# A two-layer graph network on one core: the last edges of the first layer in batches of five and three units, the last batch's stages one step earlier, and a last node group of one block

## The chip, the cores and the metric

The kernel runs on one core of a Trainium2 chip. Its time is the device time of one execution in microseconds (us). The engines are PE (matrix multiply; its weight loads are listed apart as PEld), DVE (vector), ACT (activations), POOL (here: issuing gathers) and SP (issuing transfers). Each engine works through its own list of instructions in order, and an instruction waits until what it needs has been produced or released.

## The reference, cut to what matters

There are 6250 nodes with 128 features and 206250 edges, sorted by their target node; each node has 33 incoming edges on average, itself among them. Two layers are computed, each with a layer norm of `x + layer(x)` behind it.

The first layer is graph attention with 8 heads of 16:

```
m      = leaky_relu(xl[src] + xr[dst] + edge_attr @ W_e, 0.2)
logits = sum over o of m * att              # one number per edge and head
exl    = exp(logits - segment_max(logits, dst)[dst])
alpha  = exl / (segment_sum(exl, dst)[dst] + 1e-16)
out    = segment_sum(xl[src] * alpha, dst) + b_att
h      = layer_norm(x + out); y = layer_norm(h + gelu(h @ W1 + b1) @ W2 + b2)
```

The second layer gathers a row of features for every edge (`feat[src]`, made from the result of the first layer), multiplies it with filters that a small network makes from 8 scalars of the edge, and sums over the target node.

## The kernel before, in words

**Units.** The edge list is cut into units of 6 x 128 = 768 edges, NU = 269 of them (`TU`, `UE`). A unit spans at most 32 target nodes (`W`), so its sums go into a window of 32 columns of an accumulator `acc` that starts at the unit's first target, `r0[u]`. For this the sorted targets are checked on the chip at the start; otherwise a general version would run.

**Layer one, per unit** (`attention`): `load` issues 6 gathers of 128 rows of the table `fXL` on POOL (line 366) and five transfers on SP; `terms` adds the three terms of `m` in PSUM (lines 420, 423); `parts` and `logits` make the 48 logits of each edge row on DVE (436, 439, 445).

**Batches.** The maximum over the edges of a node needs the edges in a row. So units are taken in batches of up to 8, and four stages are done once for a batch: `rows` (SP fetches two mask tables `nb` and `hb`, PE turns the logits, line 462, ACT copies them to `lgt`), `peaks` (four scans on DVE, lines 471 to 477, and a carry `cr` from the batch before), `shifts` (`gd` and `sc` on DVE, 494 and 496) and `weights` (PE 506, 508 and 516; ACT takes the exponentials, 511 and 514). `fast_plan` makes the list of batches: 3, 4, 6 and then 32 of 8, each with its `end`, the step at which the logits of its last unit are there.

**Per unit again, behind its batch:** `one_hot` and `messages` multiply the gathered rows with the weights (DVE 372, 528), `sums` adds over edges (PE 538, ACT 542 and 543 copy to `sb`), `sum_up` (PE 551) and `collect` (DVE 557) add the unit's window to `acc`; the window's start is read by DVE's sequencer from memory (value_load, L597 in the trace).

**The order is written out by hand**: `attention` runs through steps k. Step k issues the gathers of unit k+2, the terms of unit k+1, and the logits of unit k. The dictionary `when` says at which step the messages of a unit are done (one unit in a step, two near the end, never more); its sums follow one step later, its `sum_up` two and its `collect` three. `rows` of a batch are done at step `end` + 1, `peaks` at `end` + 2, `shifts` and `weights` at `end` + 3, and the last batch's messages start at `end` + 3 (of other batches `end` + 4). With 269 units and the last batch 261 to 268 (`end` 268), rows, peaks and weights of the last batch fall in steps 269, 270 and 271, its messages in steps 271 to 274 (two units each), and there are steps 0 to 277.

**Node groups.** When a stretch of 256 nodes (two blocks of 128; the first group of all is one block) has all its sums, its remaining work on nodes is done by a generator, `nodes.group`, in 19 pieces that are separated by `yield`. Counting them: 1 the sums are taken out of `acc` (PE 675, 676), 2 division and adds (DVE 679 to 687), 3 and 4 layer norm (620 to 632), 5 scale and shift (693, 694), 6 transposition (665, 667), 7 and 8 two halves of the first product with gelu (702, 705), 9 the second product (710), 10 adds (713, 714), 11 and 12 layer norm, 13 adds (720 to 722), 14 and 15 layer norm, 16 transposition, 17 the product for layer two (733, 734), 18 the transfer to the table `fFEAT` (736, 737), 19 that to `fBASE` (741). Each piece is written for g blocks. `Queue.step` lets each group in flight do one piece. At most two groups are in flight (`lanes` = 2), each with one PSUM buffer of its own, and a third starts only when the older one has done its last piece. A group may start when the unit `done` has been collected. `Queue.step` is called once at the end of each step, twice from step 273 on, and after the last step until all groups are through (`nodes.rest`). The groups of before are (0, 1), (1, 2), (3, 2), ... (45, 2), (47, 2), written as (first block, blocks); the last three may start at units 248, 259 and 268.

**Layer two** (`convolution`) works on pairs of units: `fetch` gathers 12 times 128 rows of `fFEAT` on POOL (line 366 again), into two buffers; `radial` and `filters` (803, 804, 810) make the filters, `products` (822 to 831) and `sums` (848, 850) use them, `collect` (858) adds to the accumulator `acc4`. POOL clears `acc4` first (line 764), in memory that `acc` held. `finish` does the remaining work for the same list of groups, one group at a time, in 6 pieces (PE 912, DVE 915, layer norm, transfer 924).

Of the kernel before, what the change touches and what calls it, by code (L numbers as in the profile page):

```python
# [32 lines left out]
U = 8  # L33
# [8 lines left out]
G = 2  # L42
SPREAD = 6
HEAD = (3, 4)
RAW = 4
ENDING = 28
EB = 8
# [9 lines left out]
def fast_plan(n, e):  # L57


    nu, _, np_ = fast_sizes(n, e)  # L60
    nb = np_ // P
    cuts = [0, *range(nb % G or G, nb + 1, G)]
    groups = [(b, c - b) for b, c in zip(cuts, cuts[1:])]
    done, need = [], [0] * nu
    for b, g in groups:
        q = min((b + g) * P / n, 1.0)
        u = min(nu - 1, int((q * e + SPREAD * math.sqrt(e * q * (1 - q))) / UE + 0.5))
        done.append(u)
        if u + 1 < nu:
            need[u + 1] = max(need[u + 1], (b + g) * P)  # L70
    head = HEAD if nu > sum(HEAD) else ()
    left = nu - sum(head)
    rest = (left % U,) if left % U else ()
    batches, u, end = [], 0, -2
    for m in head + rest + (U,) * (left // U):
        u += m
        end = max(u - 1, end + 2)
        batches.append((u - m, m, end))
    return groups, done, need, batches
# [28 lines left out]
class Fast:  # L108
# [269 lines left out]
    def attention(self, acc, xlp, xls):  # L378
# [3 lines left out]
        tc, nc, a, NU = self.tc, self.nc, self.a, self.NU  # L382
        with ExitStack() as st:
# [65 lines left out]
            def rows(b):  # L449

                v, m, _ = self.batches[b]
                R = m * H
                nb = b1.tile([R8, UE + 1], BF16, name="nb")
                nc.sync.dma_start(nb[:R], raw(self.NBG, v * (UE + 1), [[UE + 1, m], [0, H], [1, UE + 1]]))
                hb = b1.tile([R8, UE], BF16, name="hb")
                nc.sync.dma_start(hb[:R], raw(self.HBG, v * UE, [[UE, m], [0, H], [1, UE]]))
                lgt = b1.tile([R8, UE], F32, name="lgt")
                for t0 in range(0, TU, 4):
                    n = min(4, TU - t0)
                    ps = mp.tile([R8, 512], F32, name="m")  # L460
                    for k in range(n):
                        nc.tensor.transpose(ps[:R, k * P:(k + 1) * P], lgs[b][:, t0 + k, :R], self.ident)
                    nc.scalar.activation(lgt[:R, t0 * P:(t0 + n) * P], ps[:R, :n * P], AF.Copy)
                ws[b] = R, nb, hb, lgt

            def peaks(b):

                R, nb, hb, lgt = ws[b]
                up = b2.tile([R8, UE], F32, name="up")
                h = UE // 2  # L470
                nc.vector.tensor_tensor_scan(up[:R, :h], nb[:R, :h], lgt[:R, :h], -BIG, op0=OP.add, op1=OP.max)
                nc.vector.tensor_tensor_scan(up[:R, h:], nb[:R, h:UE], lgt[:R, h:], up[:R, h - 1:h],
                                             op0=OP.add, op1=OP.max)
                pk = b1.tile([R8, UE], F32, name="pk")
                nc.vector.tensor_tensor_scan(pk[:R, h:][:, ::-1], nb[:R, h + 1:][:, ::-1], up[:R, h:][:, ::-1], -BIG,
                                             op0=OP.add, op1=OP.max)
                nc.vector.tensor_tensor_scan(pk[:R, :h][:, ::-1], nb[:R, 1:h + 1][:, ::-1], up[:R, :h][:, ::-1],
                                             pk[:R, h:h + 1], op0=OP.add, op1=OP.max)

                c_ps = mp.tile([R8, 1], F32, name="m")  # L480
                L, last = ws["last"]
                nc.tensor.matmul(c_ps[:R], self.ident[:L, L - H:L - H + R], last, start=True, stop=False)
                nc.tensor.matmul(c_ps[:R], self.sh1[:R, :R], up[:R, UE - 1:], start=False, stop=True)
                cr = b1.tile([R8, 1], F32, name="cr")
                nc.scalar.activation(cr[:R], c_ps[:R], AF.Copy)
                ws["last"] = R, up[:R, UE - 1:]
                ws[b] = R, hb, pk, cr

            def shifts(b):

                R, hb, pk, cr = ws[b]
                gd = b1.tile([R8, UE], F32, name="gd")
                for s in (slice(0, UE // 2), slice(UE // 2, UE)):
                    nc.vector.scalar_tensor_tensor(gd[:R, s], hb[:R, s], cr[:R], pk[:R, s], op0=OP.add, op1=OP.max)
                sc = b2.tile([R8, 1], F32, name="sc")
                nc.vector.tensor_scalar(sc[:R], cr[:R], gd[:R, 0:1], 0.0, op0=OP.subtract, op1=OP.min)
                nc.scalar.activation(sc[:R], sc[:R], AF.Exp)
                sd = b2.tile([R8, U], F32, name="sd")
                nc.scalar.activation(sd[:R], self.bmask[:R], AF.Copy, scale=sc[:R])
                ws[b] = R, gd, sd  # L500

            def weights(b):
                R, gd, sd = ws[b]
                lg = lgs.pop(b)
                ex_ps = mp.tile([P, TU, R], F32, name="m")
                nc.tensor.matmul(ex_ps, self.ident, lg[:, :, :R], start=True, stop=False)
                for t in range(TU):
                    nc.tensor.matmul(ex_ps[:, t, :], gd[:R, t * P:(t + 1) * P], self.negi[:R, :R],
                                     start=False, stop=(t == TU - 1))
                ex = b2.tile([P, TU, R8], F32, name="ex")  # L510
                nc.scalar.activation(ex[:, :, :R], ex_ps, AF.Exp)  # L511
                for i in range(R // H):
                    xv = xls[self.batches[b][0] + i].rearrange("p t (h o) -> p t h o", o=OW)
                    nc.scalar.activation(xv[:, :, :, O], ex_ps[:, :, i * H:(i + 1) * H], AF.Exp)
                s_ps = mp.tile([P, U], F32, name="m")
                nc.tensor.matmul(s_ps, self.e128[:R], sd[:R], start=True, stop=True)
                s = b2.tile([P, U], F32, name="s", bufs=3)
                nc.scalar.activation(s, s_ps, AF.Copy)  # L518
                ws[b] = ex, s
# [37 lines left out]
                nc.vector.scalar_tensor_tensor(v, v, ws[b][1][:, i:i + 1], nds.pop(u), op0=OP.mult, op1=OP.add)  # L557


            when, ready, k = {}, 0, 0  # L560
            for u in range(NU):
                end = self.batches[of[u][0]][2]
                k = max(k, end + (4 if end < NU - 1 else 3))
                busy = {k - 2, k - 3} & {b[2] for b in self.batches}
                if len(when.get(k, ())) == (2 if k >= NU or k > NU - ENDING and not busy else 1):
                    k += 1
                when.setdefault(k, []).append(u)

            AHEAD = 2
            ends = {end: b for b, (_, _, end) in enumerate(self.batches)}  # L570
            for u in range(min(AHEAD, NU)):
                load(u)
                places(u)
# [2 lines left out]
            for k in range(max(when) + 4):  # L576
                now, sums_of, ups_of, got = (when.get(k - i, []) for i in range(4))
                if k + AHEAD < NU:
                    load(k + AHEAD)
                if k == 2:  # L580
                    nodes = Queue(self.nodes(st, acc), self.done, 2)
                if k + 1 < NU:
                    terms(k + 1, 0)
                if ups_of:
                    sum_up(ups_of)
                if k + 1 < NU:
                    terms(k + 1, 1)
                if k - 3 in ends:
                    shifts(ends[k - 3])
                    weights(ends[k - 3])  # L590
                if k - 2 in ends:
                    peaks(ends[k - 2])
                for u in sums_of:
                    sums(u)
                if k < NU:
                    parts(k)
                cs = [nc.vector.value_load(self.r0[0:1, u:u + 1], min_val=0, max_val=self.n) for u in got]  # L597
                if k + AHEAD < NU:
                    places(k + AHEAD)
                if k < NU:  # L600
                    logits(k)
                for u, c in zip(got, cs):
                    collect(u, c)
                for u in now:
                    ohs[u] = self.one_hot(wk, u)
                    messages(u)
                if k - 1 in ends:
                    rows(ends[k - 1])
                for _ in range(1 + (k > NU + 3) if k > 1 else 0):
                    nodes.step(max(got, default=-1))  # L610
            nodes.rest()
# [1025 lines left out]
```

## Time and profile before

| | |
|---|---|
| median of 7 executions | 4364.17 us (4356.77 to 4368.38) |
| the profiled execution | 4372.05 us, of which the span from first to last instruction is 4369.7 us |
| mean granted clock of PE | 0.857 |
| busy share of the span | PE 79%, PEld 62%, DVE 60%, ACT 22%, POOL 75% |
| gathers of layer one (`fXL`) | 1590, issued from 45.4 to 2237.0 us |
| gathers of layer two (`fFEAT`) | 1614, issued from 2331.5 to 4348.8 us |

Times in the views are microseconds from the start of the span. "Busy" is the time of the instructions themselves; issuing transfers from SP and ACT does not count, the issue of a gather on POOL does. Where a view says what ended an engine's idle time, that is inferred from semaphores; "issue" stands for time in which the engine waited for nothing that the profile shows.

### The profile page before, as it was taken

What the parts mean: (1) busy time and instruction counts of PE and PEld (TensorE: products, weight loads), DVE (VectorE), ACT (ScalarE), POOL (GpSimd) and SP (SyncE); (2) the same over time, 40 slices, a digit from 0 to 9 for tenths busy, and PEclk for the clock granted to TensorE, in tenths of its full rate; (3) what the DMA queues carried; (4) which work ended last, traced back from release to release, by engine and by line L of the source; (5) the groups of instructions that cost most, each with busy time, mean ns of one, the idle gap of its engine ahead of it and who ended that gap; (6) DMA issues with size and microseconds to landing.
All of it is one profiled execution on the core that took longest, in us unless ns stands there. A gap on an engine that the chain in (4) does not pass through costs nothing.

```text
span 4369.7 us, 67647 instructions
## 1 busy us (share of the span) xinstructions
PE 3451.3 (79%) x21381; PEld 2727.0 (62%) x21381; DVE 2643.5 (60%) x6828; ACT 963.8 (22%) x2528; POOL 3276.5 (75%) x3236
## 2 busy tenths in 40 slices
PE   6877777777777777777777888888888888888887
PEld 4666555655565666556655766666666666666666
DVE  5876676666676666666764555555555555555554
ACT  3122222222222222222232111111121121121121
POOL 6777777777777777777736777777777777777776
PEclk8977887788877787777877899999999999999998
DMA  7644444444444444444521222222222222222222
GB/s 223 182 129 127 132 126 126 127 123 135 128 124 125 128 132 133 127 124 121 142 60 49 62 61 62 61 63 62 61 62 62 57 66 59 60 63 62 61 62 51
DMA packets 290621, 428.25 MB, mean 98 GB/s; under 512 B 122700, under 2 KB 199454, under 8 KB 290254
## 3 DMA queue, kind: packets, MB, share of 16 engines
q0 software_dynamic: 103296, 218.27, 20.5%
q1 hardware_dynamic: 183258, 197.74, 15.2%
q10 hardware_dynamic: 3700, 7.82, 0.5%
q8 instruction: 173, 2.83, 0.3%
q14 instruction: 194, 1.59, 0.1%
HBM read 403.55 MB, written 19.96 MB: 97 GB/s over the span
## 4 chain that ended last, share of the span: by engine, by line
POOL 29%; PE 23%; DMA 20%; issue 15%; DVE 11%; ACT 2%; DVEq 1%; ACTq 0%; POOLq 0%; SPq 0%
POOL f L366 17%; POOL xl L366 12%; DMA xl<-fXL,fsrc 10%; DMA f<-fFEAT,fsrc 9%; PE z L420 5%; PE z L423 3%; PE y L850 2%; DVE f L831 2%; PE h_ps L803 2%; PE m L538 2%; PE w L810 2%; PE m L551 1%; DVE os L822 1%; PE y L848 1%; PE ps L912 1%
## 5 line engine op out<-in xcount | busy, mean ns | idle before, releaser
L366 POOL DMA_INDIRECT xl<-fXL,fsrc x1590 | 1708.4, 1074 | 487.1 <-issue 404.5
L366 POOL DMA_INDIRECT f<-fFEAT,fsrc x1614 | 1523.8, 944 | 509.5 <-issue 436.9
L850 PE MATMUL y<-os,f 128*128 128x96 f32 x3228 | 739.4, 312 | 10.6
L848 PEld LDWEIGHTS y<-os,f 128*128 128x128 f32 x3228 | 524.7, 198 | 314.8 <-DVE f L831 256.8
L827 DVE TENSOR_TENSOR f<-w,f 128x256 f32<-128x256 f32 x405 | 171.2, 423 | 874.7 <-DMA f<-fFEAT,fsrc 724.7
L848 PE MATMUL y<-os,f 128*128 128x32 f32 x3228 | 559.7, 256 | 139.6 <-DVE f L831 138.6
L420 PE MATMUL z<-fw,ea 128*128 128x136 f32 x3228 | 622.8, 340 | 53.1 <-DVE pr L439 43.9
L423 PE MATMUL z<-xl,fcst 128*128 128x408 f32 x538 | 320.8, 686 | 386.2 <-DMA xl<-fXL,fsrc 381.1
L804 ACT ACTIVATE h<-h_ps 128x384 f32<-128x384 f32 x540 | 265.2, 491 | 1611.4 <-PE h_ps L803 1611.1
L420 PEld LDWEIGHTS z<-fw,ea 128*128 128x128 f32 x3228 | 536.6, 237 | 102.3 <-DVE pr L439 47.8
L850 PEld LDWEIGHTS y<-os,f 128*128 128x128 f32 x3228 | 508.4, 199 | 32.9 <-DVE f L831 31.2
L822 DVE SCALAR_TENSOR_TENSOR os<-at,fl,e 128x128 f32<-128x128 f32 x1614 | 451.3, 341 | 63.4 <-PE y L850 63.1
L810 PE MATMUL w<-wq,h 128*128 128x256 f32 x1620 | 468.1, 415 | 0.0
L831 DVE TENSOR_TENSOR f<-w,f 128x384 f32<-128x384 f32 (+1 forms) x810 | 408.3, 545 | 0.0
L423 PEld LDWEIGHTS z<-xl,fcst 128*128 128x128 f32 x538 | 101.1, 235 | 413.0 <-issue 329.5
L810 PEld LDWEIGHTS w<-wq,h 128*128 128x128 f32 x1620 | 299.7, 206 | 27.6 <-issue 1.2
L803 PE MATMUL h_ps<-e,m 128*128 128x384 f32 (+1 forms) x540 | 246.2, 539 | 86.4 <-ACT h L804 76.6
L538 PE MATMUL m<-xl,oh 128*32 128x136 f32 x3228 | 226.8, 349 | 72.5 <-ACT s L518 55.5
L528 DVE TENSOR_TENSOR xl<-xl,ex 128x384 f32<-128x384 f32 x538 | 273.8, 548 | 4.0 <-ACT ex L511 4.0
L551 PEld LDWEIGHTS m<-fcst,sb 128*128 128x128 f32 x1076 | 206.6, 243 | 111.4 <-issue 105.3
L436 DVE TENSOR_TENSOR pr<-z,xl 128x408 f32<-128x408 f32 x269 | 154.6, 575 | 200.4 <-DMA xl<-fXL,fsrc 95.2
L445 DVE TENSOR_REDUCE lg<-pr 128x48 f32<-128x816 f32 x269 | 266.5, 991 | 1.6 <-DVE pr L439 1.6
(145 smaller groups left out, 4003.2 us busy)
## 6 DMA issues: line engine op xcount, KB each, us to landing
ea<-fast_eat_dram SPq DMA_DIRECT2D x269, 384.0 KB
lb<-fLB SPq DMA_DIRECT2D x269, 144.0 KB
f<-fFEAT,fsrc POOLq DMA_INDIRECT x1614
xl<-fXL,fsrc POOLq DMA_INDIRECT x1590
xr<-fXR SPq DMA_DIRECT2D x807, 8.5 KB
e<-fast_e8t_dram SPq DMA_DIRECT2D x16, 384.0 KB
fXR<-pt SPq DMA_DIRECT2D x16, 306.0 KB
fXL<-tb SPq DMA_DIRECT2D x16, 204.0 KB
```

Of the source, the lines that this page charges most:

```text
L366: self.nc.gpsimd.indirect_dma_start(out=to, out_offset=None, in_=table, in_offset=bass.IndirectOffsetOnAxis(ap=self.src[:, g:g + 1], axis=0))
L420: nc.tensor.matmul(z[:, t * ZW:(t + 1) * ZW], lhs[:, e], rhs, start=(t == 0 and lhs is ea), stop=(half == 1 and t == 2 and lhs is oht))
L423: nc.tensor.matmul(z, self.ident, xl[:, :3, :].rearrange("p t f -> p (t f)"), start=False, stop=True)
L445: nc.vector.tensor_reduce(lgs[b][:, :, i * H:(i + 1) * H], prs.pop(u).rearrange("p (t h) o -> p t h o", h=H), axis=mybir.AxisListType.X, o ...
L528: nc.vector.tensor_mul(v, v, ws[b][0][:, t:t + 3, i * H:(i + 1) * H, None].to_broadcast([P, 3, H, O]))
L538: nc.tensor.matmul(ag[q * W:(q + 1) * W], oh[:, t, :], xl[:, t, :], start=(t < 4), stop=(t + 4 >= TU))
L803: nc.tensor.matmul(ps, m, x[:, s], start=True, stop=True)
L810: nc.tensor.matmul(w[:, 2 * t:2 * t + 2, :], hs[p][:, e:e + P], wq, start=True, stop=True)
L822: nc.vector.scalar_tensor_tensor(os[:, 2 * t + i], at4, self.l[:, 2 * p + i, c * CT + t:c * CT + t + 1], e4s[p][:, 2 * (c * CT + t) + i, : ...
L831: nc.vector.tensor_mul(vy[:, :, j, 32:].rearrange("p t (c x) -> p t c x", c=3), w[:, :, None, 64 + j * 32:96 + j * 32].to_broadcast([P, n, ...
L848: nc.tensor.matmul(ys[p][:, i, 0], vy[:, e, 0], os[:, e, 3], start=(c == t == i == 0), stop=False)
L850: nc.tensor.matmul(ys[p][:, i, 1:], vy[:, e, 1], os[:, e, :3], start=False, stop=last)
```

## The change

Four edits, all in what is planned and in which step it is issued; no instruction computes anything else.

1. `TAIL = (5, 3)`: the last 8 units, 261 to 268, are two batches, 261 to 265 (`end` 265) and 266 to 268 (`end` 268). All batches before are as they were.
2. The stages are keyed by `due`, which is `end` + 1, for the last batch `end`. So all batches but the last keep their steps. The last batch has its rows in step 268, its peaks in 269 and its weights in 270; the batch of five has them in 266, 267 and 268.
3. `when` follows: the last batch's messages may start at `end` + 2, and `busy` (the steps in which only one unit's messages are placed) is the step of a batch's peaks and that of its weights. Messages: units 257 and 258 in step 266, 259 in 267, 260 in 268, then 261 and 262 in 269, and so on to 267 and 268 in step 272. There are steps 0 to 275.
4. The groups are (0, 2), (2, 2), ... (44, 2), (46, 2), (48, 1): the last is the one of a single block, in both layers. The last three may start at units 254, 264 and 268.

```
+TAIL = (5, 3)
...
-    cuts = [0, *range(nb % G or G, nb + 1, G)]
+    cuts = [0, *range((nb - 1) % G or G, nb, G), nb]
...
-    head = HEAD if nu > sum(HEAD) else ()
-    left = nu - sum(head)
+    head, tail = (HEAD, TAIL) if nu > sum(HEAD + TAIL) else ((), ())
+    left = nu - sum(head + tail)
...
-    for m in head + rest + (U,) * (left // U):
+    for m in head + rest + (U,) * (left // U) + tail:
...
-            when, ready, k = {}, 0, 0
+            when, k = {}, 0
+            due = {end + (end < NU - 1): b for b, (_, _, end) in enumerate(self.batches)}
...
-                k = max(k, end + (4 if end < NU - 1 else 3))
-                busy = {k - 2, k - 3} & {b[2] for b in self.batches}
+                k = max(k, end + (4 if end < NU - 1 else 2))
+                busy = {k - 1, k - 2} & set(due)
...
-                if k - 3 in ends:
-                    shifts(ends[k - 3])
-                    weights(ends[k - 3])
-                if k - 2 in ends:
-                    peaks(ends[k - 2])
+                if k - 2 in due:
+                    shifts(due[k - 2])
+                    weights(due[k - 2])
+                if k - 1 in due:
+                    peaks(due[k - 1])
...
-                if k - 1 in ends:
-                    rows(ends[k - 1])
+                if k in due:
+                    rows(due[k])
```

The lines of the changed file are one higher than those given here.

More of the change, by code (lines that the diff above doesn't have):

```diff
@@ L569, in attention @@
             AHEAD = 2
-            ends = {end: b for b, (_, _, end) in enumerate(self.batches)}
             for u in range(min(AHEAD, NU)):
```

## The prediction

> **What bounds the kernel now.** I start with the costliest groups of instructions, then look at POOL's waits around the middle of the span, then at the chain that ended last, there and at the end.
>
> ```profile
> L366 POOL DMA_INDIRECT xl<-fXL,fsrc x1590 | 1708.4, 1074 | 487.1 <-issue 404.5
> L366 POOL DMA_INDIRECT f<-fFEAT,fsrc x1614 | 1523.8, 944 | 509.5 <-issue 436.9
> ```
>
> Busy plus idle of the first row is 2195.5 us, of the second 2033.3. The gathers of layer one run from 45.4 to 2238.0, those of layer two from 2331.5 to 4349.7, and nearly all the idle time is 0.30 us between two gathers. So POOL is one stream with a hole of 93.5 us between the layers (2238.0 to 2331.5) and 20 us behind it. Only these two can shrink or grow; what happens beside the stream costs nothing. POOL's waits from 2200 to 2340:
>
> ```profile
> POOL acc L764 <- PE n L676: 57.2, 1, 57.2
> POOL f L366 <- DMA fBASE<-h: 15.1, 1, 15.1
> ```
>
> The hole is 57.2 us until the last node group has read `acc` (2295.1), 21.2 us of clearing `acc4` in that memory, and 15.1 us for that group's transfers. The chain through it, and behind the last gather:
>
> ```profile
> 2264.79 1.03 DVE xl L528 x2
> ...
> 2293.72 0.28 DVE acc L557
> ...
> 2310.74 3.79 PE n L710 x16
> ...
> 2327.00 4.02 DMA fBASE<-h
> ```
>
> ```profile
> 4348.80 4.13 DMA f<-fFEAT,fsrc
> ...
> 4356.04 3.78 PE ps L912 x16
> 4359.84 0.43 DVE v L915
> 4360.30 0.49 DVE st L620 x2
> ```
>
> To read: four pairs of messages from 2264.8 to 2282.4, the last collect ends at 2294.0 (T0), then 37.5 us of node work up to the first gather at 2331.5.
>
> **Part 1, the cut into 5 and 3 (up to T0): +1.4 us, bounds -4 and +5.** One batch more costs DVE four scans and `gd`, `sc`. Smaller batches are not shorter ones:
>
> ```profile
> L471 DVE TENSOR_TENSOR_SCAN up<-nb,lgt x35: 930/950/1019, 128.4 to 2253.6; 64x384 f32<-64x384 bf16 x32, 24x384 f32<-24x384 bf16 x1, 32x384 f32<-32x384 bf16 x1, 48x384 f32<-48x384 bf16 x1
> ```
>
> 24 to 64 rows all lie within 0.93 to 1.02, so a batch costs DVE 4.1 (2253.56 to 2257.66) + 1.4 = 5.5 us; PE 12 loads of `gd` of some 0.19 and their products (2.8 at 2261.4), ACT some 3. On SP the two mask transfers (0.68 + 0.58 to issue) move from step 269 into 266 and 268, behind the loads of unit 268 and ahead of `fFEAT`/`fBASE` writes that nobody waits for yet. DVE's list after 2231.3, where both versions start the messages of 257 and 258, is: messages 2.5, group 42's adds 1.35, scans 4.1, parts, loads and logits of 267 3.4, collects 0.6, message of 259 1.3, statistics 0.8, `gd` 1.4, parts and logits of 268 3.4, collects and the copy of `at4` 0.9, message of 260 1.3, group pieces 2.2. Sum 23.2: the last batch's scans start at 2254.6, not at 2253.56. The added work fills DVE's idle 3.9 (before 2241.62) and what is idle from 2248.9 to 2253.6; that cover is then used up.
>
> From there: scans 4.1, collect 1.1, messages 261/262 2.5, statistics 0.8, `gd` 1.4, end at 2264.4. PE: last products with `gd` at 2266.4 (2.8 after the first half). The exponentials must be read (2267.5) before the sums of 261 get one of the three PSUM buffers "m", and the messages of 263 wait for these sums (buffer `oh`): they start at 2268.6, with DVE idle for some 3 and group pieces and collects queued behind. Each later pair is PE's: `sum_up` 1.9, sums 2.2, copies on ACT 0.7, one 2.07 of L733. Pairs at 2274.9 and 2280.4, end 2282.9 against 2282.4. Three pairs instead of four, but started later and slower. Then sums (2285.5), L702 1.85, L675/676 1.0, division and adds 1.85, collect 1.7, statistics 0.8, adds 0.9, norm 0.4, loads and collect 1.4: T0 = 2295.4, +1.4. If two whole steps came back, at 28.6/6 = 4.8 us each (2264.8 to 2293.4 are six), it were -9.5; half of that is my low end -4; +5 is one step too late.
>
> **Part 2, the last group (T0 to the first gather): +10.2, bounds +7 and +13.** It has one block, which halves its PE and ACT work. But `Queue` holds two groups. Counting pieces by the plan: before, group 43 ends in step 275, and 47 does pieces 1 and 2 in step 277, beside the last pieces of 45. Now 44 may start only at unit 254's collect, step 267, has done 12 of 19 pieces at T0, and 46 six. Group 48 needs the lane of 44: it starts behind pieces 13 to 19 of 44 and 7 to 13 of 46. PE is slow there (3.78 for L710, 2.05 at 2288.4). In us after T0:
> - 44's statistics 0.8, 46's adds 0.9, norm 1.3, `vt` 0.35: 3.4.
> - 46: L702 2.1, gelu 0.85, then ACT loads the table for 44's square root and the gelu table again (1.28 + 0.3 + 1.28), gelu 0.85, L710 3.8: 13.9.
> - 44: L665 0.9, `vt` 0.4, L733 2.1, `ft` 0.4, L737 0.4: 18.1. Now 48 reads `acc`; clearing `acc4` ends at 18.8 + 21.2 = 40.0, in time for what follows; it is late if 48 reads `acc` 8 later.
> - 46's square root waited for `ft` on ACT (17.7 + 1.6), then norm, adds, statistics, second norm's start, 4.1: 23.4. Only now DVE divides for 48: 1.25, statistics and square root 0.8; its norm waits behind 46's `ft` (L665, `vt`, L733, `ft`: 27.7); norm, adds, L665, `vt` 1.7: 29.4.
> - 48's product chain at half width: 1.05 + 0.6 + 1.05 + 0.6 + 1.9 = 5.3, at 34.7.
> - Adds, two norms with one table load, adds, transposition, L733 1.05, `ft`: 8.2, at 42.9.
> - From the issue of `fFEAT` (2326.5) to the gather (2331.5) 5.0, half the bytes 4.8: 47.7.
>
> 47.7 - 37.5 = +10.2. On PE, what stands behind the waiting read of `acc` by 48 are 46's transposition and its L733, then all of 48; nothing else waits there. PE's clock sets the ends. Busy time by stretches, the ninth figure being the granted clock:
>
> ```profile
> 2294.00:2331.50 37.50, 15.72 (x45) 10.57 (x46) 12.52 (x51) 12.68 (x26) 21.23 (x4) 0.55 0.15 42
> ```
>
> I took durations at this clock; at the fast one L702 takes 1.1, L710 2.05, and 3 to 4 us go, which is the low end. The high end is a wait of 0.1 to 0.2 us in each of some 20 steps between engines that I left out. "ScalarE: Activation LUTs" of the Trainium skill (What ACT_TABLE_LOAD costs) speaks against the change: it adds 1.38 us of drain to a load of 1.28, so by an estimate from that page the two added switches on 46's path would cost 5.3 instead of 2.6. This trace shows no such drain: `vt` ends at 2232.58, the load starts at 2232.60, gelu at 2233.89.
>
> **Part 3, layer two: -2.8 at the end, bounds -3.4 and -2.2.** The last group of `finish` has one block: L912 x8 instead of x16 -1.9, L915 -0.2, statistics -0.3, norm -0.4; a smaller `out` transfer is the low end. Group (46, 2) now finishes in the pairs 133 and 134 instead of 130 to 132, beside the gather stream: nothing; its cover is 1.25 us per gather, and the last pair's products wait for the gather of 4348.8 (4.13) anyway.
>
> **Part 4, groups moved by a block:** (0, 2) instead of (0, 1) first. Pieces run beside gathers that never wait: nothing. Its cover gone, a group piece costs 1 to 2 us in a step.
>
> **Sum:** +1.4 + 10.2 - 2.8 = +8.8. The profiled execution took 4372.05, so 4380.9; it lies 7.9 above the median of 4364.17, so on the scale of the medians 4373.0. Bounds: -4 + 7 - 3.4 = -0.4 and +5 + 13 - 2.2 = +15.8, that is 4363.8 to 4380.0. A measurement of this kernel can tell some 0.2% (8.7 us) from no change, so my forecast sits on that line.
>
> **Rivals.**
> - **The lane wait is there, but the two steps come back in part** (T0 4.5 earlier): +10.2 - 4.5 - 2.8 = +3, 4367, no change to be seen. For it: +1.4 is a small difference of two long sums. Against it: DVE has no idle time left in 2231 to 2265. Chance 0.12.
> - **Faster: the lead of two steps carries through.** By the list above 48 alone would take 24 (0.6 to read `acc`, 42.9 - 23.4 less 2.2 of waiting for 46, and 4.8, with some gaps), so 44 and 46 add 23.7. Let T0 come 9.5 earlier and those pieces add half: -9.5 - 1.6 - 2.8 = -14, 4350. Place: what 44 and 46 still have to do at T0. With T0 that early it decides from where they add under 17. For it: they are DVE and ACT work of which some could run beside the messages. Against it: the lists of PE, DVE and ACT are in order, and pieces 13 to 19 stand behind the last collect. Chance 0.11.
> - **It doesn't do what it says:** the sorted targets must agree with the new groups' starts, or the general version runs, thousands of gathers more. The plan's margin is six deviations. Chance under 0.01.
> - **The forecast**, 0.77: of its -0.4 to +15.8, 0.48 lie above 8.7.
>
> **How the numbers follow.** The likeliest case gives 4373. Faster by over 0.2%: 0.11; within: 0.12 + 0.29 = 0.41; slower: 0.48. The range is that of the forecast with some 4 us of scatter between medians: 4360 to 4384; the faster case is left out.
>
> **What would show it.** Right: scans of 40 and 24 rows at some 0.95 us; four steps' messages from 2260 to 2283; the last collect near 2295; group 48's read of `acc` (L676 of the new file) some 18 us behind it, with PE's products for 44 and 46 between; POOL's first gather of `fFEAT` near 2343; an end 17 us behind the last gather. Wrong: a last collect before 2290, or 48's read of `acc` within 10 us of it, or clearing `acc4` as the last wait before the first gather of layer two. The gathers of layer one should end where they did.

## The result, and the profile after

The changed kernel took **4375.03 us** (median of 13 executions, 4365.51 to 4383.48) against 4363.72 (33 executions, 4354.82 to 4370.19) of the kernel before on the same chip: ratio **1.0027**, 95% interval 1.0020 to 1.0035: slower by 0.27%. Forecast were 4373.0 us and +8.8; measured is +11.3 between the medians. The profiled execution took 4379.16 us, its span is 4377.4, its clock 0.847. The two profiled executions lie only 7.1 us apart: that of before took 8.3 more than the median, that of the changed kernel 4.1 more.

POOL's two rows in the list of the costliest groups (busy and mean ns, then idle time and what ended it):

```profile
L367 POOL DMA_INDIRECT xl<-fXL,fsrc x1590 | 1708.2, 1074 | 486.8 <-issue 401.8
L367 POOL DMA_INDIRECT f<-fFEAT,fsrc x1614 | 1522.9, 944 | 503.0 <-issue 445.6
```

Busy plus idle is 2195.0 and 2025.9 (before 2195.5 and 2033.3): the streams did not change. The second row's idle shrank by 6.5 because POOL's last wait in the hole did, as the waits of POOL between 2200 and 2350 show:

```profile
POOL acc L765 <- PE n L677: 77.0, 1, 77.0
POOL f L367 <- issue: 9.7, 5, 8.5
```

The wait for `acc` grew from 57.2 to 77.0, the one behind the clearing shrank from 15.1 to 8.5: the hole went from 94.5 us (2237.03 to 2331.50) to 107.6 (2236.32 to 2343.97). PE's timeline around the end of the last collect (T0 = 2296.5), with the idle time before each row in brackets:

```profile
2289.26 1.13 PE L703 MATMUL n<-vt,w 128*128 128x256 f32 x4 [0.29 <-ACT gt L706]
2290.22 0.97 PE L552 MATMUL m<-fcst,sb 128*128 128x32 f32 x8
2291.32 2.05 PE L711 MATMUL n<-w,gt 128*128 128x128 f32 x16
...
2302.35 2.08 PE L703 MATMUL n<-vt,w 128*128 128x256 f32 x4 [0.93 <-ACT gt L706]
2306.11 3.79 PE L711 MATMUL n<-w,gt 128*128 128x128 f32 x16 [1.68 <-ACT gt L706]
2309.68 0.63 PE L666 MATMUL n<-fcst,h 128*128 128x128 f32 x2
2310.79 1.83 PE L734 MATMUL n<-wfs,vt 128*128 128x256 f32 x4 [0.47 <-ACT vt L668]
2313.55 0.39 PE L676 MATMUL n<-fcst,acc 128*128 128x8 f32 x2 [0.93 <-DVE h L738]
```

To read: the last row is group 48 reading `acc`, 17.1 us behind T0. The first product L711 is 44's, ahead of T0; everything between T0 and the last row is the rest of 46's feed-forward part and of 44, at about half the speed (L711 takes 3.79 instead of 2.05). Only when 44 has ended does 48 get its lane. The chain behind the last gather of layer two:

```profile
4360.31 4.06 DMA f<-fFEAT,fsrc
...
4367.48 2.09 PE ps L913 x8
4369.60 0.30 DVE v L916
```

From the last gather to the issue of the `out` transfer 11.39 us pass (before 13.86); the transfer itself takes 5.7 (before 7.0).

### The profile page after: what moved, and what is told of

It is laid out like the page before. It is cut to its first block, busy times and chain, and to the rows that moved or that the text cites. A ratio compares the mean times of both kernels' runs of the same rounds, so it can differ in the third digit from the quotient of the medians.

```text
span 4377.4 us, 67725 instructions
## 1 busy us (share of the span) xinstructions
PE 3494.9 (80%) x21407; PEld 2755.5 (63%) x21407; DVE 2648.2 (60%) x6835; ACT 966.3 (22%) x2536; POOL 3275.3 (75%) x3236
## 3 DMA queue, kind: packets, MB, share of 16 engines
q1 hardware_dynamic: 183258, 197.74, 15.1%
## 4 chain that ended last, share of the span: by engine, by line
PE 27%; POOL 25%; DMA 20%; issue 14%; DVE 11%; ACT 2%; DVEq 1%; SPq 0%; POOLq 0%; ACTq 0%
POOL f L367 16%; DMA xl<-fXL,fsrc 10%; POOL xl L367 9%; DMA f<-fFEAT,fsrc 8%; PE z L421 6%; PE z L424 4%; PE y L851 3%; PE h_ps L804 2%; DVE f L832 2%; PE m L539 2%; PE w L811 2%; PE m L552 2%; DVE os L823 2%; PE y L849 1%; PE ps L913 1%
## 5 line engine op out<-in xcount | busy, mean ns | idle before, releaser
L539 PE MATMUL m<-xl,oh 128*32 128x136 f32 x3228 | 231.7, 354 | 71.9 <-ACT s L519 57.7
L552 PEld LDWEIGHTS m<-fcst,sb 128*128 128x128 f32 x1076 | 208.2, 245 | 108.8 <-issue 104.8
```

The costliest lines, as they stand in the source:

```text
L539: nc.tensor.matmul(ag[q * W:(q + 1) * W], oh[:, t, :], xl[:, t, :], start=(t < 4), stop=(t + 4 >= TU))
L552: nc.tensor.matmul(nd[:, i, j], sb[:, j], self.s4, start=True, stop=True)
```

## The experiments

**The theories.** Theory A is the forecast's: group 48 needs the lane of 44, so its chain starts behind what 44 and 46 still have to do. Rival B: 48's own chain, or the work of the three groups as a whole, sets the hole, whoever waits for whom. Rival C: the cut alone is what costs. Each kernel was compared with the kernel before on the same chip. One of the three series ran on a chip where before takes 4366 us, close to the 4364 of the result (called P; whether it is the chip of the result is not on record), the others on two chips where it takes 6041 and 6034 us (Q and R); there the hole can be read, but the rest of the time is set by PE, as the last section shows. The kernels of experiments 1, 2 and 5 ran on P and Q, the changed one again on R. The ratios with their intervals need not be the quotients of the medians that stand beside them. In all tables T0 is the end of the last collect; "G" is the first gather of layer two.

**1. The changed kernel with the groups of before**, on chips Q and P.

```
-    cuts = [0, *range((nb - 1) % G or G, nb, G), nb]
+    cuts = [0, *range(nb % G or G, nb + 1, G)]
```

> The changed kernel with the node groups of before: (0, 1), (1, 2), ... (47, 2); batches and steps stay changed. T0 is the end of the last collect. Theory A (the last group waits for the lane of group 44; the cut into 5 and 3 costs little): group 47 starts right at T0, since 43 is through in step 275; it is mixed with ten pieces of group 45 instead of six, so T0 to the first gather of layer two is 40 to 41 us (before 37.5, changed 47.5); last gather of layer one to T0 stays near 60; 20.9 us behind the last gather. In all some +6 us against before, faster than the changed kernel by some 5. Theory B (the cut and the moved stages are what costs, the groups are harmless): T0 to first gather stays at 47 and the kernel is 13 to 15 us slower than before, since it also loses the shorter end.

> The changed kernel with the groups of before (last group of two blocks, 47), cut and earlier stages kept. Theory (the lane wait of group 48 costs some 10 us, the cut some 3): the wait is gone, so from the last collect (T0) to the first gather of layer two 37 to 41 us, as before (37.5) and not 47.5; last gather of layer one to T0 about 60 as in the changed kernel (before 57); end behind the last gather 20.9 as before. Sum against before: +3.2 for T0, +0 to +3: ratio 1.0005 to 1.0015. Rival (the cut makes all of the loss, and the groups none): T0 to gather 45 or more and ratio 1.003.

Chip Q: 6050.65 against 6040.95 us, ratio 1.0011 (0.9998 to 1.0024). Chip P: 4367.12 against 4366.21, ratio 1.0010 (1.0001 to 1.0019). T0 to G is 39.6 and 39.8. So the cut and the earlier stages alone do not make the whole loss on chip P, where by the ratio they cost 4.4 us (0.4 to 8.3): against rival C as the only cause. Two things were missed. T0 came 53.2 us behind the last gather on chip P, where 60 was expected; this is taken up below. And group 47, which should have read `acc` right at T0, read it 6.0 us behind T0 on both chips: on PE's list the read stands behind two products of group 45 (L703 and L711).

**2. Before with the new groups alone** (the `cuts` line of the change, nothing else).

> The kernel before with the changed node groups alone: (0, 2), ... (46, 2), (48, 1). Theory A: T0 as before within 2 us; group 44 still has three pieces left at T0, so group 48 reads acc some 11 us behind T0, the first gather follows T0 by some 42 (before 37.5); 17.1 behind the last gather instead of 20.9; in all +0 to +3 us, no change to be seen. Theory B: the one-block group is simply shorter: T0 to first gather 33 or less, the kernel 7 to 9 us faster than before.

> Before with the new groups only (batches and stages of before). Theory: last gather to T0 57 as before; 44 has 16 of its 19 pieces behind it at T0 instead of 12, so group 48 reads acc some 11 us behind T0 and T0 to the first gather is 39 to 42 (before 37.5, changed kernel 47.5); end behind the last gather 17.1 instead of 20.9. Sum -2 to +1: ratio 0.9995 to 1.0005. Rival (the groups alone make the whole of +10 in the hole): T0 to gather 47, ratio 1.0015 or more.

Ratio 0.9997 (0.9984 to 1.0011) on chip Q; 4363.00 against 4366.21, ratio 0.9991 (0.9982 to 1.0000), on P. 48 reads `acc` 10.8 and 12.1 us behind T0 (expected 11), T0 to G is 39.3 and 40.6 (39 to 42). POOL's waits on chip P:

```profile
POOL acc L764 <- PE n L676: 68.2, 1, 68.2
POOL f L366 <- DMA fFEAT<-ft: 6.4, 1, 6.4
```

The new groups alone lengthen T0 to G by 3.1 us and the hole by 2.3, which the shorter end gives back. **Neither half of the change costs what both cost together.**

**3. The earlier stages alone**, without cut and with the groups of before (chip Q).

```
-TAIL = (5, 3)
+TAIL = ()
...
-    cuts = [0, *range((nb - 1) % G or G, nb, G), nb]
+    cuts = [0, *range(nb % G or G, nb + 1, G)]
```

> The changed kernel with the groups of before and without the cut: a last batch of eight, 261 to 268, whose stages come one step earlier (277 steps). Theory A: without the extra batch's 5.5 us of DVE work the saved step comes back in part: last gather of layer one to T0 is 54 to 57 us (before 57.0, changed 60.2), T0 to first gather 38 to 39, in all -2 us against before (-5 to +2). Theory B (moving the stages forward is itself what delays T0, because rows and scans then stand ahead of the work that they overlapped with): last gather to T0 59 to 61, in all +3 to +5.

Ratio 1.0001 (0.9988 to 1.0013), T0 to G 38.0: nothing to be told from no change. The figures expected for T0 are those of a faster chip, and there is no profile of before on Q. But experiment 1, on the same chip, differs from this kernel by the cut alone: T0 lies 102.6 us behind the last gather there and 96.6 here.

**4. The changed kernel without the cut**: earlier stages and new groups (chip R), and the changed kernel itself beside it.

```
-TAIL = (5, 3)
+TAIL = ()
```

> The changed kernel without the cut: the last batch keeps its 8 units, its stages come a step earlier, and the groups are the new ones. By the plan 44 has 14 of 19 pieces behind it at T0 (12 in the changed kernel, 16 with the groups alone). If the steps taken away are what leaves the pieces behind T0: T0 to the first gather 43 to 45, between 40.6 and 47.5, last gather to T0 56 to 58, end 17.1 to 18.3: 0 to +5, ratio 1.000 to 1.0012. Rival (it is the batch added by the cut): as with the groups alone, T0 to the gather 40 to 41 and ratio 0.999.

> The changed kernel once more, unaltered, for the scatter of one profile: the granted clock in the stretch from the last gather of layer one to T0 was 0.51 and 0.64 in its first profile. If T0 hangs on the clock that this execution happened to get, last gather to T0 lies anywhere from 54 to 61; if it hangs on the plan, within 1 us of 60.2. T0 to the first gather 46 to 49 in both cases; ratio 1.0027.

6027.35 (without the cut) and 6042.96 (with it) against 6034.00 us, ratios 0.9990 (0.9978 to 1.0001) and 1.0010 (0.9998 to 1.0021). T0 to G is 44.8 without the cut (expected 43 to 45) and 46.1 with it, against 39.3 with the groups alone (experiment 2, on chip Q); 48 reads `acc` 12.6 and 15.9 us behind T0, against 10.8. So one step less before T0, which leaves two pieces of 44 more behind it, goes with 5.5 us more, and two steps go with 6.8. The order is that of theory A: **the shorter tail takes away steps in which 44 would have been finished.** The sizes are not clean, since PE's granted clock between T0 and G was 0.54 and 0.57 here and 0.63 in experiment 2.

The whole time, however, went as the rival had it: 0.9990 without the cut, where 1.000 to 1.0012 was expected. The two kernels of this experiment differ by the cut alone, and their medians lie 15.6 us apart. Of the difference in the profiles 11.1 us lie ahead of T0 (last gather to T0 is 91.8 and 102.9) and only 1.3 behind it. So on chip R the cut is dear by what it does ahead of T0. This pair did not run on chip P. The repeat does not show the scatter of T0 on the faster chips, for which it was meant; its ratio was expected at 1.0027.

**5. The changed kernel with two node pieces in each of the last 22 steps**, on chips Q and P.

```
-                for _ in range(1 + (k > NU + 3) if k > 1 else 0):
+                for _ in range(1 + (k > NU - 16) if k > 1 else 0):
```

> The changed kernel with two node pieces in a step from step 254 on instead of from 273 on. Group 42 is then through at step 263, and 44 has 18 of 19 pieces done at T0, 46 has six as in the changed kernel. Theory A: group 48 reads acc some 5 to 7 us behind T0 (17.3 in the changed kernel) and the first gather follows T0 by some 41 (47.5); T0 moves by less than 3 us; the kernel is 5 to 8 us faster than the changed one, +3 to +6 against before. Theory B (the lane is not what holds group 48): T0 to first gather stays at 46 to 48.

> The changed kernel with two pieces of node work in each of the last 22 steps instead of in the last three, so that group 44 has 18 of its 19 pieces behind it at T0 instead of 12. Theory: group 48 reads acc 5 to 7 us behind T0 instead of 17, T0 to the first gather is 38 to 41 instead of 47.5, T0 itself is up to 3 us later than in the changed kernel because of the pieces on VectorE's list; end 17.1. Sum +0 to +5 against before: ratio 1.000 to 1.001. Rival (not the wait for the lane but the length of group 48's own chain sets the hole): T0 to gather stays at 47 and the ratio at 1.003.

Ratio 1.0041 (1.0023 to 1.0058) on chip Q; 4377.60 against 4366.21, ratio 1.0032 (1.0019 to 1.0045), on P: no faster than the changed kernel, where 0 to +5 us were expected. The inner part came as theory A said: 48 reads `acc` 6.9 us behind T0, T0 to G is 38.2 (changed kernel 47.5). But T0 came 68.3 us behind the last gather instead of 60.1, and on Q 113.7 instead of the 102.6 of experiment 1. POOL's waits, and the chain ahead of T0 (chip P):

```profile
POOL acc L765 <- PE n L677: 75.1, 1, 75.1
POOL f L367 <- DMA fFEAT<-ft: 9.2, 1, 9.2
```

```profile
2270.22 2.02 PE n L703 x4
...
2273.16 2.08 PE n L703 x4
2275.23 1.55 PE m L552 x8
2276.78 1.96 PE m L539 x24
2278.74 3.13 PE n L711 x16
...
2290.06 0.34 DVE h L721
...
2291.35 0.49 DVE st L621 x2
...
2298.58 0.29 DVE acc L558
```

L703, L703 and L711 are 44's pieces 7 to 9. In the changed kernel they run from 2286.3 to 2293.4, behind the last messages; here they stand between the sums of the messages (L539, L552). The place that they left just ahead of T0 is taken by 44's pieces 11 to 16, of which the last rows show two; in the changed kernel these ran behind T0. The hole is 106.5 us against 107.6: 9.3 gained behind T0, 8.2 lost ahead of it. The theory missed this; it took the steps for places with room.

**6. Groups alone with the same early pieces** (chip P; before with the `cuts` line and the edit of experiment 5).

> Before with the new groups and two pieces of node work in each of the last 22 steps; batches and stages of before. By the plan group 48 then takes a lane while the last messages run and reads acc right behind T0. Theory: T0 to the first gather 33 to 37 (before 37.5), last gather to T0 57 to 60, end 17.1 instead of 20.9: -8 to -1, ratio 0.998 to 0.9998. Rival (the pieces stand on VectorE's list ahead of the last messages): T0 5 us or more later, nothing gained or slower.

4364.62 against 4366.21 us, ratio 0.9998 (0.9988 to 1.0009). T0 to G 35.4, but T0 at 61.2 instead of 56.1: hole 96.6 against 96.7 of experiment 2. Again what was moved ahead of T0 came back there, as the rival had it.

**7. A lane of its own for group 48**, which takes the suspected wait away without moving a piece of 44 or 46: buffers of its own, PSUM from the pool of `z` and the gelu's result in a buffer of `ea`, both unused by then (chip R, with 4).

```
-        while self.next < min(n, self.first + self.lanes) and self.turns[self.next] <= u:
+        while self.next < n and (self.next < self.first + self.lanes or self.lanes == 2 and self.next == n - 1) \
+                and self.turns[self.next] <= u:
...
+                if lane is None:
+                    z = zp.tile([P, 3 * ZW], F32, name="z")[:, :math.prod(shape)]
...
-        return [group(b, g, f"n{i % 2}") for i, (b, g) in enumerate(self.groups)]
+        return [group(b, g, f"n{i % 2}" if i < len(self.groups) - 1 else None) for i, (b, g) in enumerate(self.groups)]
```

> The changed kernel, but the last group (48) has a lane, buffers and PSUM tiles of its own, so that it starts right behind the last collect (T0) beside 44 and 46, which keep 7 and 13 pieces to do. Theory (the wait for the lane makes the hole longer): group 48 reads acc 1 to 3 us behind T0 instead of 17, and T0 to the first gather of layer two is 38 to 42 us instead of 47.5; T0 stays 57 to 60 behind the last gather of layer one. Sum against before: 0 to +5, ratio 1.000 to 1.001. Rival (what 44 and 46 still have to do fills the lists of the engines, whoever waits for whom): 48 reads acc early, but T0 to the gather stays at 45 to 48 and the ratio at 1.0025.

> The new groups only (batches and stages of before), with a lane of its own for the last group. By the wait for the lane: group 48 reads acc 1 to 3 us behind T0 instead of 12, T0 to the first gather 36 to 39 instead of 40.6: 2 to 4 us less than with the groups alone, ratio 0.998 to 0.9988. By the rival (the lists are full): T0 to the gather 40 and the ratio of the groups alone, 0.999.

6032.21 (changed kernel with the lane) and 6030.99 us (groups alone with the lane) against 6034.00, ratios 1.0002 (0.9990 to 1.0014) and 0.9995 (0.9983 to 1.0008). POOL's timeline of the changed kernel on this chip, then with the lane added:

```profile
2855.16 21.23 POOL L765 MEMSET acc<- 128x6304 f32 x4 [118.50 <-PE n L677]
2884.69 0.95 POOL L367 DMA_INDIRECT f<-fFEAT,fsrc  x1 [8.30 <-issue]
```

```profile
2838.38 21.23 POOL L774 MEMSET acc<- 128x6304 f32 x4 [102.67 <-PE z L683]
2875.40 0.95 POOL L368 DMA_INDIRECT f<-fFEAT,fsrc  x1 [15.79 <-DMA fFEAT<-ft]
```

T0 lies 102.9 us behind the last gather in both. 48 reads `acc` 0.1 us behind T0 instead of 15.9, and T0 to G is **37.7 instead of 46.1** (expected 38 to 42). The granted clock over that stretch was 0.57 in both. The medians lie 10.8 us apart, though the intervals of the two ratios overlap: the gain is clear in the hole, less so in the whole time. With the groups alone the lane takes 2.4 us (36.9, against 39.3 on Q; expected 2 to 4). This tells theory A from rival B: the pieces of 44 and 46 are done in the same order, only 48 does not wait for them, and 8.4 us of T0 to G go.

**The hole on the faster chips, put together** (us; read from one trace of each kernel; before and changed are the profiles of the result, the others ran on chip P; "to `out`" is from the last gather of layer two to the issue of the `out` transfer, so that the scatter of that transfer, 4.7 to 7.4, is left out):

| kernel | last gather to T0 | 48 (47) reads `acc` behind T0 | T0 to G | to `out` | sum against before | ratio measured, as us of 4366 |
|---|---|---|---|---|---|---|
| before | 57.0 | 0.1 | 37.5 | 13.9 | | |
| changed | 60.1 | 17.1 | 47.5 | 11.4 | +10.7 | +11.8 (8.7 to 15.3) |
| 1 old groups | 53.2 | 6.0 | 39.8 | 13.9 | -1.4 | +4.4 (0.4 to 8.3) |
| 2 groups alone | 56.1 | 12.1 | 40.6 | 9.9 | -1.7 | -3.9 (-7.9 to 0) |
| 5 early pieces | 68.3 | 6.9 | 38.2 | 12.1 | +10.3 | +14.0 (8.3 to 19.6) |
| 6 groups, early | 61.2 | 0.2 | 35.4 | 11.5 | -0.3 | -0.9 (-5.2 to 3.9) |

Three stretches of one profile give the measured difference within the intervals in all rows but that of experiment 1, which lies 2 us outside. Adding the halves (experiments 1 and 2) gives +0.5; the whole is +11.8, so some 11 us are the halves' effect on each other, give or take 6 by the intervals. In the traces this effect is 13.8: 7.8 ahead of T0, 4.6 between T0 and G and 1.4 at the end. Only the middle part can be the wait for the lane; the first is not explained, and it rests on one profile of each kernel, at different clocks.

## Why the prediction was right

**Part 1, the cut (T0 +1.4, bounds -4 and +5): mis-sized, +3.2 measured.** The scans of 40 and 24 rows took 0.94 to 1.01 us, as said; the last batch's started at 2255.95 instead of 2254.6, the messages ran from 2261.34 to 2283.2 instead of 2260 to 2283, and T0 was 2296.5 instead of 2295.4. DVE's timeline has three waits on the way:

```profile
2255.95 0.95 DVE L472 TENSOR_TENSOR_SCAN up<-nb,lgt 24x384 f32<-24x384 bf16 x1 [2.97 <-ACT lgt L464]
...
2270.00 0.36 DVE L373 TENSOR_TENSOR oh<-fl,fcst 128x192 f32<-128x192 f32 x1 [3.94 <-PE m L539]
...
2289.01 0.17 DVE L680 TENSOR_SCALAR iv<-n 128x16 f32<-128x16 f32 x1 [5.31 <-PE n L677]
```

The list had DVE full up to the last scans; in fact it waited 2.97 us for the logits, which PE turned late (at a granted clock of 0.50, where before had 1.00; the rows stand in the last section). The second wait was in the working, as "some 3"; the third is group 46's read of `acc` with collects queued behind, which the working had too. What stays open is how much of the +3.2 belongs to the cut. On chip P the one kernel with the cut and the old groups had T0 at 53.2, earlier than before; there the chain ahead of T0 holds DVE's statistics instead of L703 and L711. PE's granted clock from the last gather to T0 was 0.66 in that run, 0.67 in before and 0.57 in the changed kernel. On Q and R the pairs that differ by the cut alone have T0 later by 6.0 us (experiments 3 and 1) and 11.1 (experiment 4) with it. One profile of each can't part the plan's share from the clock's. (In the bounds of the prediction, half of -9.5 is -4.8 and not -4; nothing hangs on it.)

**The rival "faster", T0 9.5 earlier**, and the one of 4.5 earlier, did not come: in the changed kernel T0 is 3.2 later, and with the cut and the old groups 3.8 earlier (experiment 1), which the end of the hole gives back in part (39.8 against 37.5). The steps had no room for more: node pieces that were moved into them delayed T0 by 8.2 and 5.1 us (experiments 5 and 6).

**Part 2, the lane wait (+10.2): right, +10.0.** 48 read `acc` at T0 + 17.1 (forecast 18.1), the first gather came at 2343.97 (forecast 2343), and clearing `acc4` was not the last wait. The granted clock from T0 to the first gather was 0.56, as taken (0.55). Experiment 7 shows the mechanism by taking the wait away: on chip R T0 to G fell from 46.1 to 37.7, against 37.5 in before. Experiments 2 and 4 go with it: 40.6 (on Q 39.3), 44.8 and 46.1 for 16, 14 and 12 pieces done, though the clock has a share in that. That the sum is so near is in part luck. From 48's read to the issue of its `fFEAT` transfer it took 26.8 us instead of 24.8, and from there to the gather 3.6 instead of 4.8; with the read 1.0 early the errors cancel. The two added loads of activation tables are in ACT's timeline:

```profile
2302.31 1.28 ACT L624 ACT_TABLE_LOAD   x1
2303.61 0.30 ACT L624 ACTIVATE rs<-mv,feps 128x2 f32<-128x2 f32 x1
2303.92 1.28 ACT L706 ACT_TABLE_LOAD   x1
2305.21 0.84 ACT L706 ACTIVATE gt<-n,b 128x256 f32<-128x256 f32 x2
```

They cost 2.9 us from 2302.31 to 2305.21, the square root included. "ScalarE: Activation LUTs" of the Trainium skill (What ACT_TABLE_LOAD costs) would add a drain of 1.38 to each; here each load starts within 0.02 us of the end before it, so the row was the right price.

**Part 3, the end (-2.8): right, -2.5.** L912 x16 took 3.78, L913 x8 2.09. From the last gather to the end it is 20.9 to 17.1, so -3.8, but 1.3 of that is the `out` transfer, which took 4.7 to 7.4 us in the six profiles of the table, with either size of group.

**Part 4 (0): right.** The streams of gathers were as long as before (2195.0 against 2195.5 in layer one, and 2016.3 against 2017.3 from the first gather of layer two to the last), with 1590 and 1614 gathers as before, so the general version did not run.

**The sum** of the measured terms, 3.2 + 10.0 - 2.5, is +10.7 against +11.3 between the medians and +8.8 forecast. What was short is Part 1. The two profiled spans lie 7.7 apart and not 10.7: the changed one reached its last gather of layer one 0.7 earlier, took 1.0 less for the gathers of layer two, and had an `out` transfer 1.3 shorter.

The fastest version measured on chip P was the new groups alone, 3.2 us below before between the medians, with an interval that ends at no change. On that chip neither the lane nor the kernel without the cut was tried.

## What to carry to other kernels

Steps taken out of a schedule free nothing if they were also the places where other work was being finished: count what is left undone at the new end. A queue with two lanes makes the last job wait for the last but two; whether that shows depends on how much of the older jobs lies behind the point where the last may start. And work moved out of a tail into the stretch before it is paid there if the chain to the tail's start runs through the same engines: here 9.3 us came back as 8.2.

## What the hardware showed unexpectedly

**Two chips ran the same kernel 38% slower.** Before took 6040.95 us on Q (31 executions) and 6034.00 on R (35), with a granted clock near 0.72 instead of 0.857. The gathers of layer two took as long (944 and 943 ns) and so did the clearing (21.23 us); what changed is who waits. POOL's row of layer two, in experiment 2 on chip Q:

```profile
L366 POOL DMA_INDIRECT f<-fFEAT,fsrc x1614 | 1522.6, 943 | 1629.3 <-PE y L850 1167.8
```

There POOL waits for PE's products, and 10 us at either end are worth less than 0.2%. Each of these chips was seen in one series only, and no run tells what lowered the clock there.

**In the hole PE's clock does not follow how busy PE is.** Stretches of 10 us (length, then busy time and count of PE, PEld, DVE, ACT and POOL, then the granted clock), first of before, then of the changed kernel:

```profile
2237.00:2247.00 10.00, 9.40 (x53) 7.36 (x51) 4.79 (x12) 1.49 (x6) 0.95 (x1) 0.51 0.18 25
2247.00:2257.00 10.00, 6.22 (x66) 4.98 (x65) 6.58 (x13) 3.69 (x10) 0.00 (x0) 1.00 0.18 53
```

```profile
2246.30:2256.30 10.00, 7.39 (x38) 5.23 (x37) 6.01 (x17) 3.53 (x14) 0.00 (x0) 0.50 0.01 4
2266.30:2276.30 10.00, 9.36 (x70) 7.57 (x70) 3.81 (x12) 3.91 (x15) 0.00 (x0) 0.50 0.05 14
```

"TensorE: Matmul & The Clock Gate" of the Trainium skill (What's actually happening) has full clock after some 3.4 us of sustained activity. The rows speak against that here, as far as the trace's modelled ends of matmuls tell when PE works: in the changed kernel PE is busy for all of the 10.4 us from 2268.8 to 2279.2, at 0.50, while a stretch of before that is busy for 6.22 of 10 us has 1.00. Durations agree with the granted clock (L711 takes 3.79 us at half and 2.05 at full). What the clock follows here stays open. In a stretch where 10 us decide, the times of one profile depend on which clock it met.
